# Seven block products for the support of the first layer, later stores of the first masks, and a closing moved behind the keys' differences

## Chip, cores, metric

One core of a Trainium2 chip runs the whole program. The metric is the device time of one execution in microseconds (us). Timed runs of one kernel spread over up to 0.7% (35 runs of the kernel before lie between 3391.45 and 3414.60 us), and as a run on one core has no second core to compare with, all runs here count as fast. A ratio below is the mean time of one kernel's fast runs over the mean of the other's fast runs of the same rounds, so it is not quite the ratio of the medians quoted beside it. Verdicts of faster or slower are given at 2%; everything in this study is under 1%, and 95% intervals are quoted for that reason.

## The reference, cut to what matters

```python
# x: (4096, 512), adj: (4096, 4096) of 0/1, layer 0
support = (inputs @ weight).reshape(N, H, D)          # 4 heads of 128
f1 = einsum('hnd,hdo->hn', support, weight_u)         # dot products with u and v
f2 = einsum('hnd,hdo->hn', support, weight_v)
w  = leaky_relu(f1 + f2);  attn = softmax(where(adj, w, NEG)) * mask
out = einsum('hij,hjd->hid', attn, support) + bias + inputs @ proj_w + proj_b
x  = layernorm(x + out)
# layer 1: masked attention with 8 heads of 64, keys, queries and values from x
x  = layernorm(x + masked_attention(x, adj, Wks, Wqs, Wvs, Wo))
```

## The kernel before

Names are those of the profile: PE is TensorE, ACT ScalarE, DVE VectorE, POOL GpSimd, and SP issues transfers. In this program the result of a matmul stays in its PSUM buffer until an engine has copied it out; in the changed kernel TensorE once stood 8.24 us for such a copy.

The first stage goes through 8 groups of 512 rows, 4 row blocks ("steps") each. In a step TensorE makes the support block and the base block (`inputs @ proj_w`), 4 matmuls of 512 columns each, and turns a quarter of the next group's features. ACT copies the support out of PSUM, DVE makes the dots with u and v, POOL adds the bias and, at a group's end (`factors`), scales the rows.

```python
for c in range(NCJ):      # masks of the first 1024 rows, 8 blocks, beside the steps
    beside[3*c + 1] += narrow(0, c)            # POOL issues a transfer f32 -> bf16 in DRAM
    beside[3*c + 6] += turn_in0(0, c)          # SP issues a transposing transfer into `stage`
    beside[3*c + 8] += shrink(0, c, 0..1)      # ACT: bf16 -> fp8
    beside[3*c + 9] += shrink(0, c, 2..3)
    beside[3*c + 10] += keep(0, c)             # SP stores the block for layer two
...
for g in range(NG):
    ... gpsimd: x += bias ...
    for t in range(GT):
        for fn in beside.get(i, []): fn()
        s_ps = op.tile(...)                    # pool "op": 6 PSUM buffers
        for c in range(KC): matmul(s_ps, xT[:, c, t], w_sb[c])
        b_ps = op.tile(...)
        for c in range(KC): matmul(b_ps, xT[:, c, t], pw_sb[c])
        turn_x(g + 1, t)
        scalar.activation(s4[:, t], s_ps, Copy)
        for k in range(2): vector: prod = s4[:, t] * uv[:, k]; f = reduce(prod)
        vector: base = b_ps + x;  sync: store base
    factors(g, s4)                             # its transposition runs three steps later
```

The aggregation follows: for four blocks of 1024 rows and four heads, 32 steps each of a "front" (ACT and DVE make the weights p) and 8 matmuls. The masks of the next rows are narrowed, transposed and shrunk beside it. After it come the closing of rows (`add_base`, `close`: bias and projection added by a transfer, then normalisation) and layer two, whose keys, queries and values are already made by seven products of blocks. Each engine is given its instructions in program order.

## Time and profile before

| | before |
|---|---|
| timed median, range | 3408.15 us (3405.31 to 3411.09, 3 runs) |
| profiled span | 3392.6 us |
| TensorE busy | 3362.1 us, 99% |
| first stage ends (first product of the aggregation) | 247.4 us |
| ACT's wait for masks in the first stage | 47.8 us |
| TensorE's waits for ACT's copies there | 1.6 us |
| layer two starts (product 2 of the keys) | 1174.6 us |

To read it: TensorE is the bound, so only what changes its work or its gaps changes the time. The wait of ACT is large and costs nothing; that it costs nothing rests on buffers, which is easy to overlook. How far the profiled run stands for the timed ones is a question that the experiments come back to.

### The profile page before, as it was taken

How to read it: one execution, taken by the hardware profiler on the slowest of the kernel's cores; microseconds unless marked ns; L12 is line 12 of the kernel's file. 1: busy time of each engine (PE TensorE's matmuls, PEld its weight loads, DVE VectorE, ACT ScalarE, POOL GpSimd, SP SyncE). 2: the span in 40 equal slices, each digit the busy share in tenths (PEclk: the TensorE clock that was granted, in tenths of full speed). 3: DMA queues.
4: the chain of work that ended last, by engine and by line, in shares of the span. 5: the costliest groups of instructions: out<-in, count | busy, mean ns of one | idle time of the engine just before them, and what ended most of it. 6: DMA issues, size and time to landing. Idle time of an engine off the chain costs nothing.

```text
span 3392.6 us, 65576 instructions
## 1 busy us (share of the span) xinstructions
PE 3362.1 (99%) x26802; PEld 1886.3 (56%) x26802; DVE 2343.0 (69%) x2436; ACT 1986.6 (59%) x2461; POOL 2180.7 (64%) x1554
## 2 busy tenths in 40 slices
PE   9999999999999999999999999999999999999998
PEld 4449999999999855553333333333333333333332
DVE  4469899898899721147676767666666766767676
ACT  1236787877876421146665656656566665656564
POOL 3330012030030175569999999999999999999996
PEclk9999999999999999999999999999999999999999
DMA  8988959959561163278989988889888889898884
GB/s 193 227 177 146 188 132 211 185 130 222 135 163 63 32 204 124 104 212 195 210 193 222 234 203 198 197 208 231 213 198 205 198 197 256 190 212 193 202 199 110
DMA packets 397127, 620.34 MB, mean 183 GB/s; under 512 B 165520, under 2 KB 242576, under 8 KB 395792
## 3 DMA queue, kind: packets, MB, share of 16 engines
q0 software_dynamic: 97376, 258.50, 41.8%
q1 hardware_dynamic: 298912, 356.49, 35.8%
q8 instruction: 213, 3.49, 0.4%
q10 hardware_dynamic: 528, 1.05, 0.1%
q14 instruction: 98, 0.80, 0.1%
HBM read 315.87 MB, written 117.64 MB: 128 GB/s over the span
## 4 chain that ended last, share of the span: by engine, by line
PE 83%; issue 9%; POOL 3%; DMA 3%; DVE 1%; ACT 0%; SPq 0%; POOLq 0%; DVEq 0%; ACTq 0%
PE o_ps L1195 24%; PE s_ps L916 24%; PE o_ps L865 21%; PE s_ps L998 6%; PE s_ps L1259 3%; PE s_ps L991 3%; DMA p<-p 1%; POOL q_sum L1170 1%; PE o_ps L728 1%; PE o_ps L734 1%; POOL x_sb L717 1%; DMA stage<-adj_d 1%; PE s_ps L1214 1%; POOL s L664 0%; PE x_ps L846 0%
## 5 line engine op out<-in xcount | busy, mean ns | idle before, releaser
L1170 POOL TENSOR_TENSOR q_sum<-q_sum,p 128x1024 f32<-128x1024 f32 x538 | 1374.1, 2554 | 65.7 <-DMA p<-p 41.9
L1150 DVE TENSOR_TENSOR p<-s_ps,adjT 128x1024 f32<-128x1024 f32 x896 | 1043.5, 1215 | 468.3 <-ACT s_ps L1147 435.8
L1147 ACT ACTIVATE s_ps<-s_ps 128x1024 f32<-128x1024 f32 x1021 | 967.2, 1007 | 596.5 <-PE s_ps L916 593.9
L916 PE MATMUL s_ps<-q_sb,k_sb 64*64 64x512 f32 x8192 | 943.2, 589 | 1.3 <-DVE p L1150 1.3
L1195 PE MATMUL o_ps<-p,v_sb 64*64 64x512 f32 x8192 | 943.6, 590 | 0.0
L865 PE MATMUL o_ps<-sup_t,p 128*128 128x129 f32 x8192 | 919.1, 275 | 1.7 <-issue 1.7
L865 PEld LDWEIGHTS o_ps<-sup_t,p 128*128 128x128 f32 x8192 | 916.9, 192 | 1.7 <-issue 1.7
L616 DVE SCALAR_TENSOR_TENSOR p<-fr_t,dj,az 128x1024 f32<-128x1024 f32 x512 | 652.1, 1284 | 80.2 <-PE o_ps L865 53.0
L607 ACT ACTIVATE z<-fr_t,f 128x1024 fp8e4<-128x1024 f32 x512 | 558.2, 1144 | 127.4 <-DVE az L611 127.1
L916 PEld LDWEIGHTS s_ps<-q_sb,k_sb 64*64 64x64 f32 x8192 | 312.4, 133 | 568.2 <-issue 453.4
L1195 PEld LDWEIGHTS o_ps<-p,v_sb 64*64 64x64 f32 x8192 | 310.1, 133 | 570.8 <-issue 560.6
L1180 POOL DMA_DIRECT2D p<-p x412 | 438.6, 1304 | 10.0 <-PE o_ps L1195 8.4
L829 POOL DMA_DIRECT2D agg<-base_d x32 | 28.5, 1198 | 517.0 <-ACT agg L816 517.0
L1150 DVE TENSOR_TENSOR p<-s_ps,md 128x1024 f32<-128x1024 f32 x128 | 150.7, 1216 | 67.4 <-ACT s_ps L1147 64.1
L611 DVE TENSOR_TENSOR az<-adjT,z 128x512 int32<-128x512 int32 x256 | 175.4, 685 | 6.7 <-ACT z L607 6.2
L567 POOL COPY seen<-token 128x1 f32<-128x1 f32 x24 | 14.1, 587 | 252.3 <-DVE token L565 252.3
L580 ACT ACTIVATE adjT<-stage 128x1024 fp8e4<-128x1024 bf16 x128 | 130.7, 1050 | 60.5 <-DMA stage<-adj_d 60.5
L1005 ACT ACTIVATE sb<-s_ps 128x1024 f32<-128x1024 f32 x35 | 35.8, 1023 | 193.5 <-PE s_ps L998 122.5
L1020 POOL TENSOR_TENSOR sb<-sb,sb 128x1024 f32<-128x1024 f32 x36 | 84.1, 2349 | 75.5 <-ACT sb L1005 75.5
L728 PE MATMUL o_ps<-w_sb,xT 128*128 128x512 f32 x256 | 115.6, 594 | 2.1 <-ACT s L738 1.6
L742 DVE TENSOR_TENSOR prod<-s,uv 128x512 f32<-128x512 f32 x64 | 49.4, 772 | 97.6 <-ACT s L738 97.6
L734 PE MATMUL o_ps<-pw_sb,xT 128*128 128x512 f32 x256 | 115.1, 592 | 0.0
(130 smaller groups left out, 1982.6 us busy)
## 6 DMA issues: line engine op xcount, KB each, us to landing
p<-p POOLq DMA_DIRECT2D x412, 512.0 KB, 9.2
k_sb<-k_d SPq DMA_DIRECT2D x128, 512.0 KB, 7.9
v_sb<-v_d SPq DMA_DIRECT2D x128, 512.0 KB, 6.3
adj_d<-in_adj_dram POOLq DMA_DIRECT2D x32, 1024.0 KB, 15.0
sup_t<-sup_d SPq DMA_DIRECT2D x120, 258.0 KB, 8.2
adjT_d<-adjT SPq DMA_DIRECT2D x32, 512.0 KB, 4.5
fr_t<-fr_d SPq DMA_DIRECT2D x16, 1024.0 KB, 6.3
adjT<-adjT_d SPq DMA_DIRECT2D x32, 512.0 KB, 7.3
```

The source lines that it names most:

```text
L607: nc.scalar.activation(z[:, k, :], fr[:, 0, :], AF.Sign, bias=fs[j // GT][:, 0, (j + k) % GT, h:h + 1], saturate=False)
L611: nc.vector.tensor_tensor(az.bitcast(I32), adjT[w, j // CJ][:, j % CJ:j % CJ + 2, :].bitcast(I32), z.bitcast(I32), op=ALU.bitwise_and)
L616: nc.vector.scalar_tensor_tensor(p, fr[:, 1, :], dj[j // GT][:, j % GT, h:h + 1], az_t[w, h, j // 2][:, j % 2, :], op0=ALU.max, op1=ALU.mult)
L728: nc.tensor.matmul(s_ps, xT[:, c, t * P:(t + 1) * P], w_sb[c], start=(c == 0), stop=(c == KC - 1))
L865: nc.tensor.matmul(o[t // BK][:, t % BK, :], p[:, t * P:(t + 1) * P], s, start=(j == 0 and t % BK == 0), stop=(j == NT - 1), skip_group_ch ...
L916: nc.tensor.matmul(s[c:c + MS, e, :], k[r, a + c:a + c + MS], qt[g, m][r, :], start=True, stop=True)
L998: nc.tensor.matmul(half, a[:, c, n * P:(n + 1) * P], x[:, c, :], start=not more and c == 0, stop=c == 1, skip_group_check=True)
L1147: nc.scalar.activation(s, s, AF.Exp)
L1150: nc.vector.tensor_tensor(p, s, keep[:, None, :].to_broadcast([P, HP, G]), op=ALU.mult)
L1170: nc.gpsimd.tensor_tensor(q, q, p, op=ALU.add)
L1180: later.at(2, lambda: nc.gpsimd.dma_start(a, b, accum_op=ALU.add))
L1195: nc.tensor.matmul(o[c, n, :], v[r, j % CH, c], p[r, e, :], start=(j == 0), stop=(j == NT - 1))
```

## The change

The intent: seven products of half-size blocks in place of eight save an eighth of the support's matrix work in groups 1 to 7; the stores of the first masks leave a stage whose transfers are dense; the first closing no longer holds up the differences that product 3 of the keys needs.

```diff
+            def combine_x(g):           # five sums of feature blocks, on DVE, at the group's start
+            def block_product(g, s4, xT, i):
+                if i in (1, 2, 3, 6): tiles[i] = op.tile([P, G], F32, name="o_ps")
+                else: tiles[i] = tiles[{4: 2, 5: 3, 7: 1}[i]]     # 4, 5, 7 accumulate
+                more = i in (4, 5, 7)
+                ... 4 matmuls of 256 columns, start=not more and t == 0 and c == 0 ...
+                if i in (1, 2, 3): nc.scalar.activation(sb[i], out, AF.Copy)   # before 7, 4, 5
+                if i == 3: nc.gpsimd.tensor_tensor(sb[3], sb[3], sb[2], op=ALU.subtract)
+                elif i in (4, 5): nc.scalar.activation(s_block(...), as_block(out), AF.Copy) ...
+                elif i == 1: ... two sums on POOL ...
+                elif i in (6, 7): nc.vector.tensor_tensor(s_block(...), out, sb[...], op=ALU.add)
+                if i in (4, 5, 6, 7): dots(...)
...
-                    s_ps = op.tile([P, G], F32, name="o_ps")
-                    ... 4 matmuls of 512 columns ...
+                    if g:
+                        for n in ((2,), (3, 4), (5, 1), (6, 7))[t]:
+                            block_product(g, s4, xT, n)
...
-                beside.setdefault(3 * c + 10, []).append(lambda c=c: keep(0, c))
+                        if w == 0 and u == 20 + 5 * c:
+                            keep(0, c)
...
-            for _ in range(3 + WT):
+            for _ in range(2 + WT):
                 later.step()
```

More of the change, by code (lines that the diff above doesn't have):

```diff
@@ L545, in tile_gat_then_masked_attention @@
     later = Later()
+    order = (2, 3, 4, 5, 1, 6, 7)
+    of_weights = {1: ((0, 0), (1, 1), ALU.add), 2: ((1, 0), (1, 1), ALU.add),
+                  5: ((0, 0), (0, 1), ALU.add), 6: ((1, 0), (0, 0), ALU.subtract),
+                  7: ((0, 1), (1, 1), ALU.subtract)}
+    of_features = {1: ((0, 0), (1, 1), ALU.add), 3: ((0, 1), (1, 1), ALU.subtract),
+                   4: ((1, 0), (0, 0), ALU.subtract), 6: ((0, 0), (0, 1), ALU.add),
+                   7: ((1, 0), (1, 1), ALU.add)}
+    plain_weights = {3: (0, 0), 4: (1, 1)}
+    plain_features = {2: (0, 0), 5: (1, 1)}
     with tc.tile_pool(name="l0", bufs=NG) as l0, \
@@ L707, in turn_x, with w_block, combine_w @@
                     nc.scalar.activation(dst, p.rearrange("p t r -> p (t r)"), AF.Copy)
+            w_s = wp.tile([P, 2, W], F32, name="fr_t").rearrange("p k r -> p (k r)").rearrange(
+                "p (s c e) -> p s c e", c=2, e=D // 2)
+            w_s = {i: w_s[:, n] for n, i in enumerate((2, 5, 1))}
+            def w_block(m, c):
+                return [w_sb[2 * c + k][:, m * D // 2:(m + 1) * D // 2] for k in range(2)]
+            def combine_w(i):
+                a, c, op = of_weights[i]
+                dst = [w_s[i][:, k] for k in range(2)] if i in w_s else w_block(*a)
+                for k in range(2):
+                    nc.gpsimd.tensor_tensor(dst[k], w_block(*a)[k], w_block(*c)[k], op=op)
@@ new lines, in w_of, with x_block, room @@
+            def w_of(i):
+                if i in w_s:
+                    return [w_s[i][:, k] for k in range(2)]
+                return w_block(*(plain_weights[i] if i in plain_weights else of_weights[i][0]))
+            def x_block(xT, c, n):
+                return xT[:, 2 * c:2 * c + 2, n * G // 2:(n + 1) * G // 2]
+            x_s, sb = {}, {}
+            def room(tag):
+                if tag == "p":
+                    return wp.tile([P, 2, 2, G // 2], F32, name="p", bufs=LA + 1)
+                if tag == "x_sb":
+                    return sp.tile([P, D], F32, name="x_sb", bufs=3 * GT)
+                return wp.tile([P, D], F32, name=tag)
@@ new lines, in combine_x @@
+            def combine_x(g):
+                names = (3, 4, 1, 6, 7)
+                if g == NG - 1:
+                    got = [room("x_sb").rearrange("p (c r) -> p c r", c=2) for _ in names]
+                    sb.update({i: room("x_sb") for i in (2, 3, 1)})
+                else:
+                    got = [t[:, n] for t in [room("p") for _ in range(3)] for n in range(2)]
+                    sb.update({i: room(tag) for i, tag in ((2, "z"), (3, "z"), (1, "az"))})
+                for i, dst in zip(names, got):
+                    a, c, op = of_features[i]
+                    nc.vector.tensor_tensor(dst, x_block(xTs[g], *a), x_block(xTs[g], *c), op=op)
+                    x_s[i] = dst
@@ new lines, in s_block, with as_block, dots @@
+            def s_block(s4, name):
+                m, n = int(name[0]) - 1, int(name[1]) - 1
+                return s4[:, 2 * n:2 * n + 2, 2 * m:2 * m + 2, 0:D0]
+            def as_block(t):
+                return t.rearrange("p (t h d) -> p t h d", t=2, h=2)
+            def dots(g, s4, t, hs):
+                for k in range(2):
+                    prod = sp.tile([P, D], F32, name="prod").rearrange(
+                        "p (t h d) -> p t h d", t=t.stop - t.start, d=D0)
+                    u = uv[:, k, :].rearrange("p (h d) -> p h d", h=H0)[:, None, hs, :]
+                    nc.vector.tensor_tensor(prod, s4[:, t, hs, 0:D0],
+                                            u.to_broadcast(list(prod.shape)), op=ALU.mult)
+                    nc.vector.tensor_reduce(fs[g][:, k, t, hs], prod, AX.X, ALU.add)
@@ new lines, in tile_gat_then_masked_attention @@
+            tiles = {}
+            def block_product(g, s4, xT, i):
+                if i in (1, 2, 3, 6):
+                    tiles[i] = op.tile([P, G], F32, name="o_ps")
+                else:
+                    tiles[i] = tiles[{4: 2, 5: 3, 7: 1}[i]]
+                out = tiles[i]
+                more = i in (4, 5, 7)
+                xb = x_block(xT, *plain_features[i]) if i in plain_features else x_s[i]
+                wb = w_of(i)
+                for t in range(2):
+                    for c in range(2):
+                        nc.tensor.matmul(out[:, t * D // 2:(t + 1) * D // 2],
+                                         xb[:, c, t * P:(t + 1) * P], wb[c],
+                                         start=not more and t == 0 and c == 0, stop=c == 1,
+                                         skip_group_check=True)
+                if i in (1, 2, 3):
+                    nc.scalar.activation(sb[i], out, AF.Copy)
+                if i == 3:
+                    nc.gpsimd.tensor_tensor(sb[3], sb[3], sb[2], op=ALU.subtract)
+                elif i in (4, 5):
+                    nc.scalar.activation(s_block(s4, "21" if i == 4 else "12"), as_block(out),
+                                         AF.Copy)
+                    if i == 5:
+                        nc.gpsimd.tensor_tensor(as_block(sb[2]), s_block(s4, "21"),
+                                                s_block(s4, "12"), op=ALU.subtract)
+                elif i == 1:
+                    nc.gpsimd.tensor_tensor(sb[1], sb[1], sb[3], op=ALU.add)
+                    nc.gpsimd.tensor_tensor(sb[2], sb[2], sb[3], op=ALU.add)
+                elif i in (6, 7):
+                    nc.vector.tensor_tensor(s_block(s4, "22" if i == 6 else "11"),
+                                            as_block(out), as_block(sb[1 if i == 6 else 2]),
+                                            op=ALU.add)
+                if i in (4, 5, 6, 7):
+                    m, n = {4: (1, 0), 5: (0, 1), 6: (1, 1), 7: (0, 0)}[i]
+                    dots(g, s4, slice(2 * n, 2 * n + 2), slice(2 * m, 2 * m + 2))
@@ L712, in tile_gat_then_masked_attention @@
                 xg = [xs[g * GT + t] for t in range(GT)]
-                xT = xTs.pop(g)
-                if g == 0:
+                xT = xTs[g]
+                if g:
+                    combine_x(g)
+                else:
                     nc.gpsimd.tensor_add(bb[:, 0, :], bb[:, 0, :], bb[:, 1, :])
@@ L717, in tile_gat_then_masked_attention @@
                     nc.gpsimd.tensor_tensor(xg[t], xg[t], bb[:, 0, :], op=ALU.add)
+                if g == 0:
+                    for i in (2, 5, 1):
+                        combine_w(i)
                 fs[g] = l0.tile([P, 2, GT, H0], F32, name="f")
@@ L725, in tile_gat_then_masked_attention @@
                         fn()
-                    s_ps = op.tile([P, G], F32, name="o_ps")
-                    for c in range(KC):
-                        nc.tensor.matmul(s_ps, xT[:, c, t * P:(t + 1) * P], w_sb[c],
-                                         start=(c == 0), stop=(c == KC - 1))
+                    if g:
+                        for n in ((2,), (3, 4), (5, 1), (6, 7))[t]:
+                            block_product(g, s4, xT, n)
+                    else:
+                        s_ps = op.tile([P, G], F32, name="o_ps")
+                        for c in range(KC):
+                            nc.tensor.matmul(s_ps, xT[:, c, t * P:(t + 1) * P], w_sb[c],
+                                             start=(c == 0), stop=(c == KC - 1))
                     if g + 1 < NG and t == GT - 1:
@@ L737, in tile_gat_then_masked_attention @@
                         turn_x(g + 1, t)
-                    nc.scalar.activation(s4[:, t, :, 0:D0],
-                                         s_ps.rearrange("p (h d) -> p h d", h=H0), AF.Copy)
-                    for k in range(2):
-                        prod = sp.tile([P, H0, D0], F32, name="prod")
-                        nc.vector.tensor_tensor(prod, s4[:, t, :, 0:D0],
-                                                uv[:, k, :].rearrange("p (h d) -> p h d", h=H0),
-                                                op=ALU.mult)
-                        nc.vector.tensor_reduce(fs[g][:, k, t, :], prod, AX.X, ALU.add)
+                    if g == 0:
+                        nc.scalar.activation(s4[:, t, :, 0:D0],
+                                             s_ps.rearrange("p (h d) -> p h d", h=H0), AF.Copy)
+                        dots(g, s4, slice(t, t + 1), slice(0, H0))
                     base = sp.tile([P, D], F32, name="base", bufs=4)
@@ L749, in tile_gat_then_masked_attention @@
                     later.step()
+                if g == 0:
+                    combine_w(6)
+                    combine_w(7)
+                xTs.pop(g)
                 factors(g, s4)
@@ L927, in tile_gat_then_masked_attention @@
                     load_w(dst, src, c)
-            order = (2, 3, 4, 5, 1, 6, 7)
-            of_weights = {1: ((0, 0), (1, 1), ALU.add), 2: ((1, 0), (1, 1), ALU.add),
-                          5: ((0, 0), (0, 1), ALU.add), 6: ((1, 0), (0, 0), ALU.subtract),
-                          7: ((0, 1), (1, 1), ALU.subtract)}
-            of_features = {1: ((0, 0), (1, 1), ALU.add), 3: ((0, 1), (1, 1), ALU.subtract),
-                           4: ((1, 0), (0, 0), ALU.subtract), 6: ((0, 0), (0, 1), ALU.add),
-                           7: ((1, 0), (1, 1), ALU.add)}
-            plain_weights = {3: (0, 0), 4: (1, 1)}
-            plain_features = {2: (0, 0), 5: (1, 1)}
             def spare():
```

## The prediction

> **What bounds the kernel now.** I read the page's head, then a table of stretches, then single engines' timelines. The metric is the median of the timed runs, 3408.15 us (3405.31 to 3411.09); the profiled execution spans 3392.6 us, and I use it for differences only.
>
> ```profile
> span 3392.6 us, 65576 instructions
> PE 3362.1 (99%) x26802; PEld 1886.3 (56%) x26802; DVE 2343.0 (69%) x2436; ACT 1986.6 (59%) x2461; POOL 2180.7 (64%) x1554
> ...
> PE 83%; issue 9%; POOL 3%; DMA 3%; DVE 1%; ACT 0%; SPq 0%; POOLq 0%; DVEq 0%; ACTq 0%
> ```
>
> TensorE is busy 99% of the span, and the chain of waits is TensorE for 83%: only 30 us of the whole run are gaps. A gain must take matrix work away or close one of those gaps. The next view shows the four stretches that matter: the first stage to 247.4 us, the seam into the second layer at 1175.0, and what follows (columns: PE, PEld, DVE, ACT, POOL busy; granted clock; DMA share; GB/s).
>
> ```profile
> 0.00:247.40 247.40, 238.78 (x648) 112.14 (x649) 126.50 (x202) 67.89 (x118) 83.19 (x95) 1.00 0.92 199
> 1175.00:1182.80 7.80, 3.24 (x8) 1.16 (x7) 2.33 (x6) 2.38 (x7) 7.23 (x8) 1.00 0.89 215
> ```
>
> In the first stage DVE is half idle over the whole stretch and POOL two thirds, so they look like places for extra work. What they do there is set by waits:
>
> ```profile
> L728 PE MATMUL o_ps<-w_sb,xT 128*128 128x512 f32 x256 | 115.6, 594 | 2.1 <-ACT s L738 1.6 <-DVE xT L705 0.5
> L734 PE MATMUL o_ps<-pw_sb,xT 128*128 128x512 f32 x256 | 115.1, 592 | 0.0
> L580 ACT ACTIVATE adjT<-stage 128x1024 fp8e4<-128x1024 bf16 x32 | 32.0, 1049 | 47.8 <-DMA stage<-adj_d 47.8
> ```
>
> The first row is the support product, the second the base product; TensorE waits 2.1 us for the first. The third says that ACT stood 47.8 us behind transposed masks that had not landed, yet almost none of it reached TensorE: six PSUM buffers absorbed it.
>
> The seam is one gap, and the DVE timeline there says why:
>
> ```profile
> 1174.64 3.60 PE L998 MATMUL s_ps<-xT,wk_low 128*128 128x512 f32 x8
> 1182.81 8.80 PE L998 MATMUL s_ps<-adjT,wk 128*128 128x512 f32 x16 [4.57 <-DVE adjT L966]
> ```
> ```profile
> 1180.54 0.69 DVE L507 BATCH_NORM_STATS2 bn_st<-agg 128x6 f32<-128x512 f32 x1 [5.34 <-DMA agg<-base_d]
> 1181.34 0.18 DVE L509 BATCH_NORM_AGGREGATE bn_mv<-bn_st 128x2 f32<-128x6 f32 x1
> 1181.44 2.36 DVE L966 TENSOR_TENSOR adjT<-xT 128x1024 f32<-128x1024 f32 x2
> ```
>
> The statistics of the first closing tile wait for a transfer, and the differences of features that product 3 needs stand behind them in DVE's order.
>
> [...] An f32 matmul shows as two records. [...] a support product of 8 records takes 3.43 us (429 ns), and the value product of layer two, 128x256, shows 112 records in 24.17 us (215.8 ns). Splitting columns costs almost nothing. [...] here the clock reads 0.61 at 1182.8 to 1186.3, after the 4.57 us gap. [...] The product with u and v, 0.69 us alone, took 1.02 at 225.1 while POOL scaled rows[...].
>
> **The change part by part.**
>
> Products. In groups 1 to 7 a group's support is 16 matmuls of 512 columns, 32 records x 429.2 ns = 13.73 us. It becomes 7 products x 4 matmuls of 256 columns, 56 records x 215.7 = 12.08 us. 1.65 us x 7 groups = 11.6 us less TensorE work, all of it on the path if the stage stays bound by TensorE.
>
> Added work. DVE: five sums of features at 0.66 us (the 128x512 SBUF sum of layer two) and two sums out of PSUM at 0.68, 4.7 us a group on 15.8. POOL: four sums at about 1.3 us (the bias add's 1330 ns mean), 5.2 us on 10.6. ACT: one more copy of 0.59 us. All fit beside 27.5 us of TensorE, by sums. By order they fit less well. Products 4, 5 and 7 accumulate onto tiles that ACT must first copy, and between a copy's source and that product stand only a base product (3.43), turning (0.44) and another product (1.72): 5.6 us. Before, a support tile came round again three steps later, over 18 us of slack. An ACT stopped by a mask now reaches TensorE.
>
> Mask stores. Eight 512 KB stores leave the first stage: 4.2 of its 50 MB, an estimate of 18 us at 200 GB/s for the seven before 247 us. POOL's later issues of the masks' narrowing, now behind mid-group sums, also spread what came in pairs at 49.3 and 137.6. So masks should land sooner. In the aggregation the stores have room (DMA share 0.69).
>
> Tail of the stage. From 231.5 to 247.9 DVE never paused: two steps of dot products, and the first three masks' fronts (5.1 us). Now the last two steps hold three quarters of a group's dots, not half (+2.6 us), two extra PSUM sums (+1.3), and take 0.8 us less on TensorE. TensorE's transposition of the factors, before the first aggregation, waited 0.52 us; I expect about 6, so +5.5.
>
> Seam. The differences go ahead, product 3 follows product 2, the gap of 4.57 us and the half clock after it (about 1.7 us) vanish. But the scaling of the query weights on ACT waits for a transfer until 1195.87, and the copy that product 7 needs stands behind it: 1195.87 + 1.92 + 1.02 = 1198.8, while the earlier chain would ask for it at 1195.3. Before, product 7 began near 1201.7. So I count 3 us, not 6.3.
>
> Sum: -11.6 (products) -1.5 (of the 2.1 us of old waits) -3 (seam) +5.5 (tail) +3 (copies behind masks, first differences) = -7.6 us. 3408.15 - 7.6 = 3400.5, taken as **3400**.
>
> **The rivals.**
>
> First rival: ACT behind the masks takes the place of the work. Before, masks landed 9.7, 13.9 and 10.8 us after TensorE began their steps (167.41 against 157.72, 193.62 against 179.74, 214.36 against 203.56). With 2 us of shrinking, and 7.3 or 8.6 us from step start to the accumulating product, unchanged landings would stop TensorE some 4 to 5 us three times, each with a cold clock after: 14 to 20 us, and the result is 3408 to 3415. Against it: those three followed the pair of narrowings at 137.6, which is now spread, and the stores are gone; the first ones landed 1 to 4 us late, which is harmless.
>
> Second rival: everything lies beside. Tail and copies stay hidden and the seam gives its full 6.3: 11.6 + 2.1 + 6.3 = 20 us, 3388. For it: 99% TensorE. Against it: DVE saturated at the tail.
>
> Third: DVE becomes the bound of groups 1 to 7. 15.8 + 4.7 = 20.5 of 27.5 us, even with 0.35 us more on ten instructions 24; I hold it unlikely outside the last group, though the first differences of each group (DVE free some 4 us into the group, needed at 5.6) have little slack.
>
> **Range and chances.** The two rivals' ends, 3388 and 3415, bound what I find plausible; the runs scatter by 3 us either way. I take 3389 to 3412 for 8 in 10. Two per cent is 68 us; the largest effect of either sign named here is 20. Chances: faster 0.01, within 0.98, slower 0.01.
>
> **What would show it.** Right: support records of 128x256 at a start-to-start of 215.7 ns, 11.6 us less TensorE in the first stage; TensorE's idle time in the stage mostly at one place, the factors' transposition at its end, released by ACT behind DVE's dots, 4 to 7 us; ACT's wait for masks well below 47.8 us; no gap ahead of product 3 in layer two, a short one ahead of product 7 of the keys, behind the scaling of the query weights. Wrong: gaps of several us inside groups 1 to 6, ahead of products 4, 5 or 7, released by ACT or DVE; or a first aggregation that starts straight after the stage; or new waits in the aggregation's first passes where the stores now are, which I have put at zero.

## The result, and the profile after

The changed kernel takes 3419.19 us (median of 4 runs, 3413.19 to 3426.87) beside 3406.73 us before (4 runs): ratio 1.0038, 95% interval 1.0014 to 1.0062. It is slower, clear of noise though "same" at 2%, and outside the predicted range of 3389 to 3412.

The page's head of the changed kernel, to be held against the one in the prediction:

```profile
span 3424.7 us, 66036 instructions
PE 3360.4 (98%) x26970; PEld 1925.2 (56%) x26970; DVE 2405.0 (70%) x2485; ACT 1991.0 (58%) x2468; POOL 2246.8 (66%) x1592
```

The span grew by 32.1 us, yet TensorE's busy time fell by only 1.7. The spans overstate the change: the profiled run of the changed kernel (3426.87 us) was the slowest of its four, and that of the kernel before (3394.5 us) is shorter than all four timed beside it; the medians differ by 12.5 us. TensorE's waits, longest first (what waited, who released it, us in total, times, longest), say where it stands:

```profile
PE o_ps L802 <- ACT z L807: 14.9, 2, 8.2
PE o_ps L994 <- DVE p L633: 13.5, 1, 13.5
PE o_ps L688 <- ACT fr L672: 8.3, 1, 8.3
...
PE o_ps L802 <- ACT az L807: 3.4, 2, 2.6
PE s_ps L1110 <- ACT agg L945: 1.6, 1, 1.6
PE s_ps L1110 <- ACT sb L1117: 1.3, 1, 1.3
```

L802 is the block product: 14.9 + 3.4 = 18.3 us ahead of products 4 and 7, waiting for ACT's copies of products 2 and 1. L688 is the transposition of the factors at the first stage's end. L994 is the aggregation, and the last two rows are the seam. The timelines of TensorE and of ACT around the largest of the first show the chain (start, duration, instruction, in brackets the idle time before and its releaser):

```profile
83.31 3.78 PE L802 MATMUL o_ps<-w_sb,p 128*128 128x256 f32 x8 [8.24 <-ACT z L807]
```
```profile
80.77 2.00 ACT L597 ACTIVATE adjT<-stage 128x1024 fp8e4<-128x1024 bf16 x2 [11.31 <-DMA stage<-adj_d]
82.68 0.58 ACT L807 ACTIVATE z<-o_ps 128x512 f32<-128x512 f32 x1
```

ACT stands 11.31 us in front of a mask that has not landed, shrinks it, and only then copies product 2 (`z`); TensorE starts product 4 right after that copy. The 8 records of product 4 then take 3.58 us until the base product starts, not the 1.72 us of one at full clock (245.07 to 246.79, granted clock 1.00). The granted clock (column after the busy times) of the first stage and of the 8 us around this wait shows the second cost:

```profile
0.00:267.40 267.40, 234.30 (x815) 146.87 (x815) 186.32 (x251) 71.82 (x125) 148.53 (x133) 0.96 0.89 169
83.00:91.00 8.00, 7.69 (x15) 4.63 (x16) 2.66 (x4) 3.72 (x6) 2.00 (x2) 0.60 1.22 125
```

So the first stage can be added up. It ends at 267.6 us in place of 247.4, 20.2 later. TensorE's idle time in it went from 247.4 - 238.78 = 8.6 to 267.4 - 234.30 = 33.1 us, 24.5 more. Its busy time fell by 4.5 us in place of the 11.6 of work removed; the missing 7.1 are my estimate of what the lower clock cost (the difference of those two numbers). -11.6 + 7.1 + 24.5 = 20.0, which only splits up the measured difference. The kernel called both below does the same work there at a clock of 0.99 and is busy 228.77 us; against it the lower clock cost 234.30 - 228.77 = 5.5 us, the better estimate.

The aggregation took 943.5 us (267.63 to 1211.14, where product 2's wait of 1.62 begins) against 927.2 before, mostly one gap of 13.52. Layer two, from product 2 of the keys to the end, took 2211.9 us against 2218.0. Of the 32.1 us, then, 20.2 are in the first stage, 16.3 in the aggregation, 1.6 in that wait, and layer two gives 6.1 back.

### The profile page after: what moved, and what is told of

It reads as the page before. It is cut to its first block, busy times and chain, and to the rows that moved or that the text cites. A ratio compares the mean times of both kernels' runs of the same rounds, so it can differ in the third digit from the quotient of the medians.

```text
span 3424.7 us, 66036 instructions
## 1 busy us (share of the span) xinstructions
PE 3360.4 (98%) x26970; PEld 1925.2 (56%) x26970; DVE 2405.0 (70%) x2485; ACT 1991.0 (58%) x2468; POOL 2246.8 (66%) x1592
## 4 chain that ended last, share of the span: by engine, by line
PE 86%; DMA 2%; SPq 1%; DVE 1%; issue 0%; ACT 0%; POOL 0%; POOLq 0%; DVEq 0%; ACTq 0%
PE o_ps L1307 26%; PE s_ps L1045 25%; PE o_ps L994 23%; PE s_ps L1110 5%; PE s_ps L1371 3%; PE s_ps L1103 3%; DMA stage<-adj_d 1%; SPq L591 1%; DMA wq<-in_L_gnn_Wqs_dram 1%; PE s_ps L1326 1%; PE x_ps L975 0%; DMA p<-p 0%; DVE p L1439 0%; DMA sup_t<-sup_d 0%; PE x_ps L1103 0%
## 5 line engine op out<-in xcount | busy, mean ns | idle before, releaser
L994 PE MATMUL o_ps<-sup_t,p 128*128 128x129 f32 x8192 | 923.4, 276 | 13.5 <-DVE p L633 13.5
L994 PEld LDWEIGHTS o_ps<-sup_t,p 128*128 128x128 f32 x8192 | 921.2, 193 | 13.7 <-DVE p L633 13.7
L1156 DVE COPY k_sb<-s_ps 128x1024 f32<-128x1024 f32 x12 | 14.7, 1225 | 139.5 <-PE s_ps L1110 89.8
L1371 PE MATMUL s_ps<-wo_sb,on 128*128 128x512 f32 x240 | 110.8, 604 | 0.0
## 6 DMA issues: line engine op xcount, KB each, us to landing
adj_d<-in_adj_dram POOLq DMA_DIRECT2D x32, 1024.0 KB, 14.9
```

The source lines that it names most:

```text
L994: nc.tensor.matmul(o[t // BK][:, t % BK, :], p[:, t * P:(t + 1) * P], s, start=(j == 0 and t % BK == 0), stop=(j == NT - 1), skip_group_ch ...
L1371: nc.tensor.matmul(s, on_t[g][:, m, t * P:(t + 1) * P], wo_sb[:, m, :], start=(m == 0), stop=(m == NP1 - 1))
```

## The experiments

Two theories stood first. **Lost slack:** ACT was late before as well, but a support tile could wait three steps; now products 4, 5 and 7 need a copy 5.6 us after its source, so each late mask stops TensorE, and a lower clock follows: 0.50 in the 3.6 us after each of the two longest of these stops (8.24 and 6.70 us). **Stores:** the stores of masks, moved into the aggregation, delay the next rows' masks there, and the gap of 13.5 us is the cost. The first four kernels take the change apart; the next four test what makes ACT late and what the lateness costs; the last four what is left. All twelve gave correct results. Three builds failed for want of SBUF (a third buffer for arriving masks) and two were turned down before the chip because a narrowing set at a step that never comes left a tensor unwritten; they are not runs, and the record does not list them.

### One part at a time

**after_again** is the changed kernel unaltered.

> The changed kernel once more, for a second trace. If the four waits of TensorE before products 4 and 7 in the first stage (18.3 us in the first trace) and the one before the first factors (8.3 us) belong to the change, they come again within 4 us in all. The gap of 13.5 us in the aggregation's first rows sits where the timed runs differ most (3413 to 3427), so it may be smaller here: theory 'stores' says at least 5 us each time, the rival 'chance of that run' says about none in most runs.

**only_products** puts the other two parts back:

```diff
+                beside.setdefault(3 * c + 10, []).append(lambda c=c: keep(0, c))
-                        if w == 0 and u == 20 + 5 * c:
-                            keep(0, c)
-            for _ in range(2 + WT):
+            for _ in range(3 + WT):
```

> The products alone: mask stores back in the first stage, closing back before the differences. Theory 'ACT behind the masks': the waits before products 4 and 7 stay at 15 us or grow by a few (the stores now compete as well), the tail stays at 8 us, no gap in the aggregation, the seam's 4.6 us gap is back: ratio to before 1.003 to 1.007. Rival 'the stores in the aggregation cost it': with them gone, the time falls to the kernel before or under it, ratio 0.997 to 1.000.

**only_stores** and **only_seam** are the kernel before with the one or the other of those edits made forwards.

> The kernel before with only the stores of the first rows' masks moved into the aggregation. Theory 'ACT behind the masks' says little of it: the first stage gains at most the 2 us of its old waits, ratio 0.999 to 1.001. Theory 'stores' expects the gap of some 13 us in the aggregation to appear here too, with transposes of the second rows' masks landing later: ratio 1.002 to 1.005.

> The kernel before with only the first closing behind the differences. Predicted 3 us less, 6.1 us read from the first trace of the changed kernel (layer two from its first product: 2211.9 us against 2218.0): ratio 0.9980 to 0.9993, no gap before product 3, one of 1 to 4 us before product 7 of the keys.

Measured, all beside 35 runs of before (median 3404.98 us):

| kernel | median us | ratio, 95% interval |
|---|---|---|
| after_again | 3427.72 | 1.0066 (1.0051 to 1.0081) |
| only_products | 3422.96 | 1.0066 (1.0049 to 1.0084) |
| only_stores | 3406.60 | 1.0007 (0.9994 to 1.0019) |
| only_seam | 3402.57 | 0.9995 (0.9984 to 1.0006) |

The products alone cost what the whole change costs. The first stage's waits are the same again: 14.7 + 3.6 us before products in after_again, 14.9 + 0.3 in only_products, and 8.3 and 8.4 before the factors. The trace of only_products is of the fastest of its six runs (3409.18 us; the others took 3421.80 to 3434.30) and has no gap in the aggregation. In it ACT waited 50.4 us for masks in the first stage, hardly more than the 41.8 to 47.8 of the three traces whose first stage is that of the kernel before (before, only_seam, before_narrow6); yet TensorE stopped for 15.2 us. The stores and the seam are within 0.2% of nothing. The rival that the stores explain the time is out.

The gap in the aggregation needs care. TensorE's timeline of only_seam, where first stage and aggregation are those of the kernel before:

```profile
386.93 3.84 PE L865 MATMUL o_ps<-sup_t,p 128*128 128x129 f32 x32 [1.24 <-DVE p L616]
391.15 14.56 PE L865 MATMUL o_ps<-sup_t,p 128*128 128x129 f32 x128 [0.39 <-DVE p L616]
413.46 111.69 PE L865 MATMUL o_ps<-sup_t,p 128*128 128x129 f32 x976 [7.75 <-DVE p L616]
```

It has 9.4 us of gaps there without any moved store, and its aggregation takes 938.0 us. The kernel before seems to fall into this gap in most executions, though no trace of one of its longer runs was kept: of its 35 runs, 11 lie between 3391 and 3399 us and 24 between 3401 and 3415. Its profiled run (3394.5 us, not one of these) is as short as the 11. after_again has the gap again, 13.4 us, as the theory of the stores asked for; but a gap without moved stores says that the 13.5 us in the changed kernel are mostly not the change's; against only_seam its aggregation is 5.5 us longer, and which part of the change does that was not separated. only_stores, with 10.9 us of gaps in its trace and a ratio that cannot be told from 1, speaks against the stores as a large part.

The seam alone did what was predicted in the trace and gave it back. In only_seam product 3 follows product 2 at once, and product 7 waits:

```profile
1187.65 3.60 PE L998 MATMUL s_ps<-xT,wk_low 128*128 128x512 f32 x8
1191.09 7.03 PE L998 MATMUL s_ps<-adjT,wk 128*128 128x512 f32 x16
...
1212.29 3.70 PE L998 MATMUL s_ps<-adjT,adjT 128*128 128x512 f32 x8 [3.87 <-ACT sb L1005]
```

The wait of 4.57 us went, and one of 3.87 took its place: the copy that product 7 needs, behind the query weights' scaling on ACT. From product 2 of the keys to its end only_seam takes 0.6 us less than the kernel before (2217.4 against 2218.0), not the 6.1 that the expectation had read from the changed kernel, and its ratio missed the range of 0.9980 to 0.9993.

### What makes ACT late, and what lateness costs

Times of the transposing transfers on SP's queue (how long the issue held the queue) beside the narrowing transfers on POOL's queue gave a further theory. In the changed kernel a narrowing meant for a step stands in POOL's order behind the group's sums, and so starts just as a transposition does. That the one slows the other is the theory to be tested. SP's and POOL's timelines of the changed kernel:

```profile
87.48 17.83 SPq L591 DMA_TRANSPOSE stage<-adj_d  x1
...
183.24 18.40 SPq L591 DMA_TRANSPOSE stage<-adj_d  x1
```
```profile
87.47 0.80 POOL L585 DMA_DIRECT2D adj_d<-in_adj_dram  x1
...
184.28 0.80 POOL L585 DMA_DIRECT2D adj_d<-in_adj_dram  x1
```

The same two transpositions in the kernel before, 6 and 17 us after the last narrowing, and between them one that does not fit, long though the last narrowings, a pair, were issued 10 us before it:

```profile
84.70 8.52 SPq L574 DMA_TRANSPOSE stage<-adj_d  x1
...
147.56 17.73 SPq L574 DMA_TRANSPOSE stage<-adj_d  x1
183.37 8.17 SPq L574 DMA_TRANSPOSE stage<-adj_d  x1
```

**narrow_early** issues the narrowings of a group ahead of the group's sums on POOL:

```diff
-                beside.setdefault(3 * c + 1, []).append(lambda c=c: narrow(0, c))
+                early.setdefault((3 * c + 1) // GT, []).append(c)
...
+                for c in early.get(g, []):
+                    narrow(0, c)
                 fs[g] = l0.tile([P, 2, GT, H0], F32, name="f")
```

> The changed kernel with one thing moved: the narrowing transfers of the first rows' masks are issued on POOL at the start of a group, ahead of the group's four sums, which is when the kernel before issued them. Theory 'narrowing pushed into the transposes': the transposes that took 14 to 20 us (groups 1, 2, 4, 5) are back near 8 to 10 us except the one behind a pair, ACT waits under 40 us for masks in the first stage (58 us in the changed kernel), TensorE's waits before products 4 and 7 fall from 17 us to under 8 us, and the first stage ends 8 to 14 us earlier. Rival 'it is the short slack alone': waits stay at 12 us or more.

**shrink_after** shrinks the masks after the step's products and copies, not ahead of them:

```diff
-                beside.setdefault(3 * c + 8, []).append(lambda c=c: [shrink(0, c, k) for k in (0, 1)])
-                beside.setdefault(3 * c + 9, []).append(lambda c=c: [shrink(0, c, k) for k in (2, 3)])
+                behind.setdefault(3 * c + 8, []).append(lambda c=c: [shrink(0, c, k) for k in (0, 1)])
+                behind.setdefault(3 * c + 9, []).append(lambda c=c: [shrink(0, c, k) for k in (2, 3)])
...
+                    for fn in behind.get(i, []):
+                        fn()
                     later.step()
```

> The changed kernel with one thing moved: ACT's shrinking of masks comes after the step's products and copies instead of ahead of them. Theory 'short slack': each late mask has one step (6.9 us) more before it holds a copy that TensorE needs, so waits of 8.2, 6.7 and 2.6 us fall to 4 us in all, with the long transposes still there (14 to 20 us); first stage 10 to 15 us shorter. Rival 'DVE and POOL behind ACT hold TensorE too': waits move to other products, DVE or POOL named, and the stage gains under 5 us.

**both** makes both edits.

> Both moves together. If masks are the whole of it, TensorE has no wait over 1.5 us inside the groups, its records run at full clock, and the first stage ends at 250 to 253 us (267.4 in the changed kernel, 247.4 before) with the 8.3 us before the factors left as it is; ratio to before 0.998 to 1.002. If the tail came from masks too, it shrinks as well.

**before_narrow_late** is the kernel before with narrowings 1 to 7 held back, each by a tiny POOL copy that waits for the support copy of steps 4, 6, 9, 13, 17, 18 and 22:

```diff
+                    for c in range(NCJ):
+                        if late.get(c) == i:
+                            seen = small.tile([P, 1], F32, name="seen")
+                            nc.gpsimd.tensor_copy(seen, s4[:, t, 0, 0:1])
+                            narrow(0, c)
```

> The kernel before, support as one product, with the narrowing transfers held back by tiny POOL copies to about the steps at which the changed kernel issues them. Theory 'narrowing pushed into the transposes': the transposes of the second, fifth and sixth blocks take 14 to 20 us here too, ACT waits over 60 us for masks, but TensorE, with three steps of slack, waits under 8 us and the time stays within 0.2% of before (ratio 0.999 to 1.003). If TensorE stops 15 us here as well, slack is no part of it.

Measured (before: median 3403.23 us, 67 runs); ACT's wait for masks and TensorE's wait for copies are those of the first stage:

| kernel | median us | ratio, 95% interval | ACT for masks | TensorE for copies | stage ends |
|---|---|---|---|---|---|
| the changed kernel (first trace) | 3419.19 | 1.0038 (1.0014 to 1.0062) | 58.0 | 18.3 | 267.6 |
| narrow_early | 3411.41 | 1.0030 (1.0019 to 1.0042) | 40.0 | 8.0 | 253.7 |
| shrink_after | 3408.66 | 1.0019 (1.0008 to 1.0030) | 38.5 | 6.0 | 251.7 |
| both | 3398.13 | 0.9990 (0.9975 to 1.0004) | 27.8 | 1.0 | 244.2 |
| before_narrow_late | 3408.18 | 1.0027 (1.0014 to 1.0039) | 37.9 | 0.0 | 248.0 |

The first row is from other rounds; the same kernel in after_again came to 1.0066.

Lost slack holds. The order of ACT alone, with the long transpositions still there (15 to 20 us in shrink_after), takes two thirds of TensorE's waits away (4 us had been expected to be left); narrow_early takes more than half, so how late the masks come counts as well; with both edits they are 1.0 us and the stage ends 23 us earlier than in the changed kernel. ACT's wait in the changed kernel, then TensorE's waits for ACT's copies in narrow_early (two lines) and shrink_after:

```profile
L597 ACT ACTIVATE adjT<-stage 128x1024 fp8e4<-128x1024 bf16 x32 | 32.0, 1050 | 58.0 <-DMA stage<-adj_d 58.0
```
```profile
PE o_ps L802 <- ACT z L807: 7.4, 2, 5.8
...
PE o_ps L802 <- ACT az L807: 0.5, 1, 0.5
```
```profile
PE o_ps L802 <- ACT z L807: 6.0, 3, 4.1
```

TensorE's waits in the first stage of both, all of them after the start:

```profile
PE o_ps L688 <- ACT fr L672: 6.8, 1, 6.8
PE o_ps L802 <- ACT z L807: 1.0, 1, 1.0
```

And in the kernel before, ACT waited 47.8 us for masks while TensorE waited 1.6 for ACT's copies: lateness of a like size, with three steps of slack, was free.

The theory about narrowings and transpositions came out half. In narrow_early the transpositions of groups 2 and 5 are shorter, 11.95 and 14.64 us in place of 17.83 and 18.40, but not the 8 to 10 expected, and the two that stand behind a pair stayed at 15.96 and 18.96; ACT's wait, expected under 40 us, is 40.0. In before_narrow_late both expectations missed: no transposition is over 10.7 us, and ACT waited less than before, not more; the held-back narrowings did not fall on the transpositions as they do in the changed kernel, so this run does not try lateness of that size with the long slack. It did keep TensorE free of waits for copies in the first stage; its 0.27% probably lie in the aggregation, where its trace has 14.3 us of gaps, and why was not followed up. What can be said: in the first-stage trace of the changed kernel, transpositions with no narrowing issued within 4.5 us of their start take 4 to 8 us, those with one within about a microsecond 17.8 and 18.4, those with one on either side within 4.5 us 15.6 and 19.8. The kernel before has the exception shown above, 17.73 us. That the narrowing is the cause of the long ones is possible, but not shown.

### What is left: the tail and the aggregation

The wait before the factors (6.8 to 8.4 us in all kernels with products so far) was predicted from DVE's load. DVE's timeline over the last steps of both:

```profile
214.52 6.33 DVE L768 TENSOR_TENSOR x_sb<-xT 128x512 f32<-128x512 f32 x4
...
226.17 3.32 DVE L633 SCALAR_TENSOR_TENSOR p<-fr_t,dj,az 128x1024 f32<-128x1024 f32 x2
229.41 1.75 DVE L628 TENSOR_TENSOR az<-adjT,z 128x512 int32<-128x512 int32 x1
231.19 2.17 DVE L633 SCALAR_TENSOR_TENSOR p<-fr_t,dj,az 128x1024 f32<-128x1024 f32 x1
```

The four sums of features shown take 1.6 us each where such a sum alone takes 0.66, and a front's `az` 1.75 in place of 0.68: POOL is at work at the same time, scaling rows and adding the bias from 213.01 to 223.66 us, and with two of its own sums of blocks from 228.36 to 232.28. In this trace DVE has no idle time from 205.75 us to the stage's end. **both_last_plain** makes the last group's support as one product per row block again; products 6 and 7 get weights in rooms of their own, since they had overwritten two blocks of the weights.

```diff
+            w_s.update({i: sp.tile([P, 2, D // 2], F32, name=f"w_s{i}", bufs=1) for i in (6, 7)})
...
-                if g:
+                if 0 < g < NG - 1:
                     combine_x(g)
...
-                    if g:
+                    if 0 < g < NG - 1:
                         for n in ((2,), (3, 4), (5, 1), (6, 7))[t]:
...
-                    if g == 0:
+                    if g in (0, NG - 1):
                         nc.scalar.activation(s4[:, t, :, 0:D0], ...)
```

> Both moves, and the last group's support again as one product a row block (its products' weights 6 and 7 get rooms of their own). Theory 'DVE sets the tail': DVE has five sums, two additions and one row block's dots less in the last two or four steps, the 6.8 us before the factors shrink to under 2 us, TensorE pays 1.7 us more for the plain group, and the first stage ends 4 to 7 us earlier than with both moves alone (244.2 us); ratio to before 0.996 to 0.998. Rival 'the first three fronts and POOL hold the tail anyway': the wait stays at 5 us or more.

**products_fixed** is both with stores and closing back where they were before (the edits of only_products on top of both).

> The products with both moves, but mask stores in the first stage and the closing ahead of the differences, as before: what the products are worth by themselves once masks no longer stop them. First stage 244 to 248 us, so 0 to 4 us under before, seam gap as before: ratio 0.9985 to 1.0005. If the stores matter to masks, the waits before products 4 and 7 come back (over 3 us in all) and the stage ends after 249 us.

**before_narrow6** asks what the gap in the aggregation is, in the kernel before:

```diff
-                        if u == 16 + 8 * c:
+                        if u == 4 + 6 * c:
                             narrow(w + 1, c)
```

> The kernel before with the narrowing of later rows' masks issued every 6 steps from step 4 of a pass in place of every 8 from step 16. It tests what makes the gap of 8 to 14 us in the aggregation, which runs of the kernel before show too: if the transposes are long (19 to 28 us) because narrowing transfers run beside them, they are shorter here, the gap is under 3 us and the median falls by 6 to 10 us, ratio 0.997 to 0.999. If the gap has another cause it stays, ratio 0.999 to 1.001.

**best** is both_last_plain with that edit.

> Both moves, the last group plain, and the narrowing of later rows' masks every 6 steps from step 4. If gains add up: first stage 238 to 241 us, no gap in the aggregation's first rows, layer two 6 us shorter than before: ratio to before 0.993 to 0.996. If the aggregation's gap does not depend on the narrowing, 0.996 to 0.998.

Measured (before: median 3402.11 us, 20 runs):

| kernel | median us | ratio, 95% interval | before the factors | stage ends | gap in the aggregation |
|---|---|---|---|---|---|
| both_last_plain | 3394.29 | 0.9969 (0.9956 to 0.9982) | 0.5 | 237.8 | 10.4 |
| products_fixed | 3396.04 | 0.9993 (0.9977 to 1.0009) | 6.8 | 248.5 | none |
| before_narrow6 | 3393.02 | 0.9974 (0.9960 to 0.9988) | 0.5 | 246.3 | none |
| best | 3381.99 | 0.9937 (0.9923 to 0.9952) | 0.5 | 237.5 | none |

DVE sets the tail: it never paused there in both, and with the last group plain it does pause again and the wait before the factors is 0.47 us. As the edit takes four sums off POOL as well, DVE's added work and its longer times beside POOL (1.6 us a sum in place of 0.66) are not told apart.

```profile
237.65 0.28 PE L688 MATMUL o_ps<-ident,fr 128*32 128x128 f32 x1 [0.47 <-ACT fr L672]
```

products_fixed suggests that moving the stores was right for the products: with the stores back in the first stage the waits before products are 2.2 and 1.9 us in place of 1.0 in both, and the stage ends at 248.5 in place of 244.2. That is one trace each, though: the three traces with the first stage of the kernel before end it between 246.3 and 249.7 us, and the ratios, 0.9993 and 0.9990, cannot be told apart. In the kernel before (only_stores) nothing of it is seen.

The gap in the aggregation goes in before_narrow6, and with it the upper cluster of run times: all 7 runs lie between 3389.55 and 3395.88. The fourth of its transpositions for the second rows' masks starts at 366.25 us, in only_stores at 398.34. The narrowings' timing makes this gap. The kernel before has it without the change, and it was large enough to blur every comparison here.

best adds the gains up and is 0.6% under before, the shortest of all; at 2% that is still "same". Against before_narrow6 of the same rounds, which has no gap either, it is 11.0 us shorter (no run of one reaches the range of the other), of which 8.8 are in the first stage: this is what the change is worth once mended. One expectation missed: layer two is about 2 us shorter than before, not 6 (2215.8 against 2218.0).

## Why the prediction was wrong

**The step that failed** is the first rival's dismissal and the term that stood for it, "+3 us (copies behind masks, first differences)". It measured 18.3 us of waits and an estimated 5.5 to 7.1 of lower clock. The mechanism was named, at 14 to 20 us ("3408 to 3415"), and then set aside with "So masks should land sooner" and the argument that narrowings which came in pairs would be spread. They were spread, into the transpositions' time, and masks did not land sooner: ACT's wait for them rose from 47.8 to 58.0 us (50.4 in only_products). The prediction treated a change of issue times as a relief, without setting the new times beside those of the transfers that they would meet. shrink_after and both show that this was the term. That the rival's size came out close is partly luck: it counted three late masks in groups 5 and 6 and called the first ones harmless, but of the 18.3 us, 8.2 fell in group 2 and 2.6 in group 3, behind those first ones.

**Products, -11.6 us.** The size of the work was right. A block product in the changed kernel takes 1.72 us for 8 records at a granted clock of 1.00 (245.07 to 246.79), 215 ns each; the prediction had counted 215.7, and the trace before gives 215.8 (112 records in 24.17 us). In both, TensorE is busy 228.77 us up to the stage's end at a clock of 0.99, 10.0 less than before. In the changed kernel the lower clock (0.96 over the stage) hid more than half of it: busy time fell by 4.5. "All of it on the path if the stage stays bound by TensorE" was the right condition, and it did not hold.

**Tail, +5.5 us.** Right in mechanism, small in size: 8.3 - 0.5 = 7.8 us. The prediction's terms for the last two steps (2.6, 1.3 and 0.8) leave out the last group's five sums of features. In the changed kernel DVE never paused from 225.49 us, before these sums, to the stage's end, so they belong to the tail, and with POOL beside them they took 7.0 us, not five times 0.66. In the kernel before the wait was 0.52 us:

```profile
247.32 0.28 PE L671 MATMUL o_ps<-ident,fr 128*32 128x128 f32 x1 [0.52 <-ACT fr L655]
```

The sums of features in the changed kernel, those of groups 1 to 6 (`p`) and those of the last group (`x_sb`):

```profile
L768 DVE TENSOR_TENSOR p<-xT 128x512 f32<-128x512 f32 x30 | 38.1, 1332 | 0.0
...
L768 DVE TENSOR_TENSOR x_sb<-xT 128x512 f32<-128x512 f32 x5 | 7.0, 1457 | 0.0
```

**Seam, -3 us.** Right in mechanism, open in size: alone the ratio is 0.9995 with an interval that holds 0 and 3 us, its trace shows 0.6 us, and that of the changed kernel 4.5 (6.1 less a new wait of 1.6). A wait ahead of product 7 appeared where it was expected (3.9 us alone, 1.3 with the products). Not foreseen is a wait of 1.6 us ahead of product 2 that all kernels with products in every group from 1 to 7 have (1.1 in the two whose last group is plain); it was not explained.

**Stores, 0 us.** Not to be told from zero alone (0.9994 to 1.0019).

**Old waits, -1.5 us.** Gone, as said; they were too small to matter.

**Third rival, DVE as the bound of the groups.** Not seen inside the groups beyond 1.3 us: 0.3 released by `x_sb` in the last group's first sums, and 1.0 by copies of turned features (0.5 before). At the tail of the last group it holds, as the prediction allowed.

One more lesson on the base: the profile that the prediction was read from came from the faster cluster of the kernel before, so a gap of about 10 us, which by only_seam and before_narrow6 most of its runs seem to have, was not in it. It cancels in the ratio only as long as both kernels have it equally often.

## What to carry to other kernels

A wait may cost nothing only because of a buffer, as ACT's 47.8 us here; before giving accumulating products a shorter way from source to reuse, look up which late transfer stands in the same engine's order and count the slack again. Put work that waits for a transfer behind the copies that the bound engine needs (that alone took TensorE's waits for copies from 18.3 to 6.0 us here), and set every transfer that a change moves beside the ones that it will now meet. When timed runs form two clusters, find out which one the profile belongs to before reading small gaps from it.

## What the traces show of clock, transposing transfers and sums

- A wait was followed by a lower granted clock in some cases and not in others. In after_again a wait of 2.44 us was followed by 0.58 (132.3 to 136.0); in the first trace of the changed kernel one of 2.62 us at the same place was followed by 1.00 (131.6 to 135.3), those of 8.24 and 6.70 us by 0.50 (83.31 to 86.90 and 180.12 to 183.70). In the kernel before, 4.57 us at the seam were followed by 0.61 (1182.8 to 1186.3). The length of the wait alone does not separate these cases.
- One and the same transposition took very different times in one execution of the changed kernel: its issue held the queue 3.97 us at its shortest (230.21, DMA share 0.86 meanwhile) and 19.83 at its longest (155.67, share 1.19). Two that took 7.51 and 8.00 us had a share of 1.28, so the share does not order them.
- DVE's sums of features took 1332 ns on average in groups 1 to 6 of the changed kernel, 680 to 1752, against 658 to 683 for the same shape in layer two of the kernel before. The five of group 2 (70.38 to 77.35, 1.4 us each) run while POOL scales rows and adds the bias (69.51 to 79.69); the sum that starts at 109.56, just before POOL's scaling, took 0.68. That POOL is the cause was not tested.
